# Two graph layers on one core: earlier transposes, copies graph by graph, distance rows on one engine, gates divided anew

## The chip, the cores and the metric

The kernel runs on one core of one Trainium2 chip. The metric is the device time of one execution in microseconds, the median of several. A core has four engines that compute, each with its own queue that is worked off in order: TensorE (PE in the profile, with PEld for the loading of its weights), VectorE (DVE), ScalarE (ACT) and GpSimd (POOL). SyncE (SP) issues most of the DMA transfers; ScalarE and GpSimd issue some too. An engine that waits for a semaphore holds up everything behind it in its queue.

## The reference

There are 64 graphs of 256 nodes with 256 features each, all float32. Layer 0 normalises the adjacency by the degrees, multiplies it with the features and a weight, and ends in a residual and a layer norm. Layer 1 has three branches on the result x: a convolution branch with 17 taps along the nodes, a message branch whose weights come from distances, and a gated unit (GRU) over both:

```python
h = d_inv_sqrt * adj * d_inv_sqrt + alpha_eff * I          # layer 0
x = layernorm(x + (h @ x) @ W.T + b)
c = relu(bn1(conv1x1(x)))                                   # layer 1, convolution
x_conv = relu(bn2(conv17(c)) + x)
s = x @ w_se.T + b_se                                       # layer 1, messages
A = exp(-(|s_n|^2 + |s_m|^2 - 2 s_n . s_m))
x_nmp = A @ relu(x @ w_msg.T + b_msg)
r, z = sigmoid(...), sigmoid(...)                           # layer 1, gates
n = tanh(gi_n + r * gh_n)
x = layernorm(x + (1 - z) * n + z * x)
```

## The kernel before, in words

The convolution over 17 taps is done by a discrete Fourier transform over overlapping stretches of 48 nodes, eight stretches a graph. The 64 graphs are taken in four groups of Q = 16 so that the 128 partitions are filled (16 graphs by 8 stretches). For each group four kinds of work follow one another, and work of other groups is set beside them:

- `graphs`: for each graph a generator `layer0` (two graphs ahead) and a generator `layer1`, cut into pieces by `yield`. `layer1` transposes x1 (`p_x1T`, L419) and copies it to `xn` (L420), multiplies it by the 1x1 convolution (`p_conv1`, L428) and the message weight (`p_msg`), transforms h forward (`p_dft`, L463) and copies the spectrum into the tile V (L468). Then it makes the distances: two rows are transposed into one PSUM bank (`p_rows`), `dist_l` is copied out of its lower half by ScalarE (L478) and `dist_r` out of its upper half by VectorE (L480), and `p_dist` (L487), Exp, a product with the adjacency (L489) and `p_nmp` (L494) follow. The result `xn` goes to memory. `PLACES` says after which piece of `layer1` a piece of `layer0` or of a filler ("other") is put.
- the products (`products`, L518): the spectra of V times those of the filters, on TensorE, in 12 steps. Their results overwrite V, of which M is another view.
- the inverse transform (`real_transform`, `complex_begin`, `complex_end`): on VectorE alone, in many small operations on M. `output` writes the result of each frequency pair to memory (`xc_d`, L705).
- the gates (`gates`, `gru`): for each graph the convolution result is loaded, transposed (`p_xcT`, L764), summed on GpSimd (L775 to L780), and multiplied by the gate weights (`p_rz`, L796, and `p_n`, L833).

What stands beside what is written by hand. While the products of a group run, `begin`, the first graphs of the next group, is taken a few pieces a step; as V is not free then, these AHEAD graphs (12 of the second group, 6 of the later ones) put their spectra into a second tile V2. While `complex_end` runs, `paced` puts pieces of it between the marked VectorE operations of the main work, RATES pieces for a mark:

```python
RATES = (1.2, 0.85, 0.85, 1.35)
...
run(paced(begin, end, RATES[q]))
```

After `complex_end` and the graphs ahead, four copies of ScalarE bring V2 into V (L1032), each a quarter of the frequencies of all graphs ahead at once. Then the other graphs of the group run, with the first EARLY = 4 gates of the group before as fillers; the other 12 ("late") are kept for the next products and the next inverse transform. After the last inverse transform come the 16 gates of the last group alone.

A scheduler may still move an instruction past a neighbour on its engine, so that the order of the instructions is near that of the program but not the same.

Of the kernel before, what the change touches and what calls it, by code (L numbers as in the profile page):

```python
# [14 lines left out]
P = 128  # L15
# [11 lines left out]
def kernel(  # L27
# [27 lines left out]
    nc = tc.nc  # L55
    B, N, D = x.shape
# [351 lines left out]
        nc.scalar.dma_start(x1_d[g // Q][g % Q].rearrange("(c p) d -> p c d", p=P), x1)  # L408
        yield

    def layer1(g, V, place):

        x1, adjT = X1.pop(g), ADJT.pop(g)
        xn = work.tile([P, 2 * DCH, N], F32, name="xn")
        x1T = xn[:, :DCH]
        p = bank("p_x1T").rearrange("p (k n) -> p k n", k=DCH)
        for k in range(DCH):
            for c in range(NCH):
                nc.tensor.transpose(p[:, k, c * P : (c + 1) * P], x1[:, c, k * P : (k + 1) * P], ident)  # L419
        nc.scalar.copy(x1T, p)  # L420

        yield

        h = work.tile([P, NCH, D + NSE], F32, name="h", bufs=1)
        for c in range(NCH):
            p = bank("p_conv1")[:, : D + NSE]
            for k in range(DCH):
                nc.tensor.matmul(  # L428
                    p, x1T[:, k, c * P : (c + 1) * P], wc1[:, k, :], start=k == 0, stop=k == DCH - 1
                )  # L430
            mark(nc.vector.tensor_tensor(h[:, c, :], p, bc1, op=ALU.add))
        nc.scalar.activation(h[:, :, :D], h[:, :, :D], AF.Relu)  # L432

        s3 = h[:, :, D:]
        cols = scols.rearrange("p c (q r) -> p c q r", r=32)
        nc.vector.tensor_copy(cols[:, :, :, :NSE], s3.unsqueeze(2).to_broadcast([P, NCH, 4, NSE]))
        sq3 = small.tile([P, NCH, NSE], F32, name="sq3")
        nc.vector.scalar_tensor_tensor(sq3, s3, -1.0, s3, op0=ALU.mult, op1=ALU.mult)
        nsq = small.tile([P, NCH], F32, name="nsq")
        nc.vector.tensor_reduce(nsq, sq3, AX.X, ALU.add)  # L440
        nc.vector.tensor_scalar(
            cols[:, :, 2:4, NSE], nsq.unsqueeze(2).to_broadcast([P, NCH, 2]), 0.5, None, op0=ALU.mult
        )
        yield
        msg = work.tile([P, NCH, D], F32, name="msg", bufs=1)
        p = bank("p_msg").rearrange("p (c d) -> p c d", c=NCH)
        for c in range(NCH):
            for k in range(DCH):
                nc.tensor.matmul(  # L449
                    p[:, c, :], x1T[:, k, c * P : (c + 1) * P], wmsg[:, k, :], start=k == 0, stop=k == DCH - 1  # L450
                )
        mark(nc.vector.tensor_tensor(msg, p, bmsg_t.unsqueeze(1).to_broadcast([P, NCH, D]), op=ALU.add))  # L452
        nc.scalar.activation(msg, msg, AF.Relu)
        yield


        mid = GT // 2
        for k in range(DCH):
            p = bank("p_dft")

            for c, t0, t1 in ((0, 0, mid + 1), (1, mid - 1, GT)):
                first = t0 + 1 - c * mid
                nc.tensor.matmul(  # L463
                    p[:, t0 * FL : t1 * FL], h[:, c, k * P : (k + 1) * P],
                    fwd[:, first : first + t1 - t0, :].rearrange("p t f -> p (t f)"),
                    start=c == 0, stop=True, skip_group_check=c == 1,
                )
            nc.scalar.copy(  # L468
                V[:, :, k, place * GT : (place + 1) * GT],
                p[:, : GT * FL].rearrange("p (t f) -> p f t", f=FL),  # L470
            )

        yield
        p = bank("p_rows")
        for c in range(NCH):
            nc.tensor.transpose(p[:, c * P : (c + 1) * P], scols[:, c, :], ident)
        dl = work.tile([64, N], F32, name="dist_l", bufs=1)
        nc.scalar.copy(dl, p[0:64, :N])  # L478
        dr = work.tile([64, N], F32, name="dist_r", bufs=1)
        nc.vector.tensor_copy(dr, p[64:P, :N])  # L480
        yield

        aT = work.tile([P, NCH, 2, P], F32, name="aT", bufs=1)
        for c in range(NCH):
            rows = slice(32 * c, 32 * c + 32)
            p = bank("p_dist")[:, :N]
            nc.tensor.matmul(p, dl[rows, c * P : (c + 1) * P], dr[rows, :], start=True, stop=True)  # L487
            nc.scalar.activation(aT[:, c].rearrange("p n q -> p (n q)"), p, AF.Exp, bias=nsq[:, c : c + 1], scale=2.0)  # L488
        mark(nc.vector.tensor_mul(aT, aT, adjT[:, :, 0:3:2, :]))  # L489
        yield  # L490
        p = bank("p_nmp").rearrange("p (k n) -> p k n", k=DCH)
        for k in range(DCH):
            for mc in range(NCH):
                nc.tensor.matmul(  # L494
                    p[:, k, :], msg[:, mc, k * P : (k + 1) * P], aT[:, mc].rearrange("p n q -> p (n q)"),
                    start=mc == 0, stop=mc == NCH - 1,
                )
        nc.scalar.copy(xn[:, DCH:], p)
        nc.scalar.dma_start(xn_d[g], xn)
        yield  # L500
# [3 lines left out]

    VM = freq.tile([P, FL, D], F32, name="VM")
    V, M = VM.rearrange("p f (k q) -> p f k q", k=DCH), VM

    def load_u(n, i):
        u = ustream.tile([P, DCH, D], F32, name="u")
# [362 lines left out]
    def chain(*stages):  # L872
        for stage in stages:
            yield from stage
# [13 lines left out]
    def run(stage):  # L888
        for _ in stage:
            pass  # L890
# [13 lines left out]
            yield  # L904


    PLACES = (("other",), ("layer0",), (), (), ("layer0",), ("other", "layer0"), ())

    def graphs(first, part, V, others):


        for i in part:
            load(first + i + 3)
            given = {"layer0": layer0(first + i + 2) if first + i + 2 < B else iter(()), "other": others[i]}
            for piece, _ in enumerate(layer1(first + i, V, i)):
                yield
                for name in PLACES[piece]:
                    if next(given[name], "end") != "end":
                        yield
            yield from given["other"]  # L920

    with tc.tile_pool(name="setup", bufs=1) as setup:
# [29 lines left out]
        more_weights = gate_weights()  # L952
        others = [weights(setup, i, scale2) for i in range(NPARTS)]
        others += [take(more_weights, 1) for i in range(NPARTS, Q)]
        run(graphs(0, range(Q), V, others))
        bih_t = setup.tile([P, 3 * D], F32, name="bih", tag="taps", bufs=2)
        nc.sync.dma_start(bih_t, bcast_rows(b_ih, 3 * D))
        bhh_t = setup.tile([P, 3 * D], F32, name="bhh", tag="taps", bufs=2)
# [4 lines left out]
        nc.vector.tensor_copy(bn_t[:, 0, :], bih_t[:, 2 * D :])  # L963
        nc.vector.tensor_copy(bn_t[:, 1, :], bhh_t[:, 2 * D :])
    ustream = ctx.enter_context(tc.tile_pool(name="ustream", bufs=6))
    EARLY = 4

    def open_ahead(graphs):

# [20 lines left out]
    def nothing():  # L990
        return iter(())

    RATES = (1.2, 0.85, 0.85, 1.35)


    scope, AHEAD, V2 = open_ahead(12)
    late = nothing()
    for q in range(NQ):
        first = (q + 1) * Q
        more = q + 1 < NQ  # L1000
        end = complex_end(q)
        if more:
            if q:
                others = [take(late, 3 if i % 3 == 0 else 2) for i in range(AHEAD)]
            else:
                others = [nothing() for _ in range(AHEAD)]
            begin = graphs(first, range(AHEAD), V2, others)
        sums(0)
        real = real_transform()
        for step in range(STEPS):  # L1010
            if step < 4:
                run(products(step))
            else:
                run(merge(products(step), take(real, 1)))
                run(complex_begin(step))
            if q:
                run(take(late, (0, 1, 1, 1, 1, 1, 2, 1, 2, 1, 2, 1)[step] if more else step % 2))
            else:
                run(take(begin, 3))
        run(real)  # L1020
        if not q:
            run(paced(begin, end, RATES[q]))
        elif more:
            run(paced(chain(merge(take(late, 20), take(begin, 6), 3), begin), end, RATES[q]))
        else:
            run(paced(late, end, RATES[q]))
            run(end)
        if more:
            run(late)
            run(end)  # L1030
            for f in range(0, FL, 12):
                nc.scalar.copy(V[:, f : f + 12, :, : AHEAD * GT], V2[:, f : f + 12])  # L1032
            if q == 0:
                scope.close()
                gate = ctx.enter_context(tc.tile_pool(name="gate", bufs=2))
            early = gates(q, range(EARLY))
            others = [take(early, 5 if q == 0 else 2) for _ in range(Q)]
            run(graphs(first, range(AHEAD, Q), V, others))
            run(early)
            if q == 0:  # L1040
                scope, AHEAD, V2 = open_ahead(6)
                ctx.enter_context(scope)
            late = gates(q, range(EARLY, Q))
        else:
            run(gates(q, range(Q)))

# [52 lines left out]
```

## Time and profile before

| | before |
|---|---|
| time, median of 3 | 2175.89 us (2173.8 to 2175.93) |
| span of the profiled execution | 2169.2 us |
| granted TensorE clock, mean | 0.99 |
| memory read and written | 200.62 and 103.06 MB, 140 GB/s over the span |
| first products start, groups 1 to 4 | 285.7, 645.1, 1161.7, 1668.0 us |
| last products end | about 389, 758, 1273, 1751 us |
| last store of the last inverse transform issued | 1901.6 us |

The busy time of an engine is the time in which it had an instruction in work. A wait line names the waiting engine, its output tile and its line, then whom it waited for, and then the total in us, how often, and the longest. A windows line gives for a stretch of time the busy us of each engine (and how many instructions), the granted clock, the share of the DMA engines and GB/s. In a timeline the first number is the start, the second the length; in brackets stands how long the engine had been idle and for whom. Most groups of matmuls count two entries for one matmul of the program, since each float32 product shows as two.

### The profile page before, as it was taken

To read this page: it belongs to the slowest core of one execution; us is meant where nothing else is said; L and a number is where in the kernel's file an instruction comes from. 1 tells how busy PE (TensorE), PEld (TensorE's weight loads), DVE (VectorE), ACT (ScalarE), POOL (GpSimd) and SP (SyncE) were. 2 spreads that over 40 slices of the span, in tenths; PEclk is the share of its full clock that TensorE was granted. 3 is DMA by queue.
4 is the path that set the end of the run, shared out by engine and by line. 5 is a ranking of instruction groups with operands and counts; after the bars stand their busy time and mean duration, and the time that the engine had idled before them with its cause. 6 is when DMAs were issued, how large, how long until landed. Compare 5 with 4: busy or idle time off the path is not lost. (4 is left out here: it accounts for less than half of the span.)

```text
span 2169.2 us, 29039 instructions
## 1 busy us (share of the span) xinstructions
PE 2062.6 (95%) x9805; PEld 1746.3 (81%) x9805; DVE 1551.3 (72%) x3691; ACT 833.2 (38%) x1847; POOL 664.0 (31%) x640
## 2 busy tenths in 40 slices
PE   6999999887999999999999999899999998999998
PEld 5788788766788887788888888778888887888887
DVE  5555568785568798775556989775555889977776
ACT  3665643455331122455453122346543112222222
POOL 2445310112331233313222133323231123444442
PEclk9999999999999999999999999999999999999999
DMA  4756666434347644344335654334334844444441
GB/s 120 235 193 195 199 192 213 144 122 146 93 117 226 195 118 122 107 124 120 103 98 179 204 167 115 110 115 133 101 98 124 249 117 122 124 122 104 113 105 55
DMA packets 251332, 305.65 MB, mean 141 GB/s; under 512 B 18324, under 2 KB 229864, under 8 KB 251184
## 3 DMA queue, kind: packets, MB, share of 16 engines
q1 hardware_dynamic: 183680, 200.46, 30.2%
q10 hardware_dynamic: 44480, 67.39, 8.7%
q0 software_dynamic: 23024, 35.95, 8.5%
q8 instruction: 78, 1.28, 0.2%
q14 instruction: 70, 0.57, 0.1%
HBM read 200.62 MB, written 103.06 MB: 140 GB/s over the span
## 5 line engine op out<-in xcount | busy, mean ns | idle before, releaser
L833 PE MATMUL p_n<-wn,inputs 128*128 128x256 f32 x1536 | 356.0, 385 | 10.8 <-DVE first L809 10.6
L796 PE MATMUL p_rz<-wrz,sums 128*128 128x256 f32 x1536 | 350.9, 382 | 3.2 <-POOL sums L775 2.3
L833 PEld LDWEIGHTS p_n<-wn,inputs 128*128 128x128 f32 x1536 | 289.2, 192 | 58.0 <-DVE first L809 14.3
L796 PEld LDWEIGHTS p_rz<-wrz,sums 128*128 128x128 f32 x1536 | 290.7, 191 | 48.1 <-issue 5.9
L796 PE MATMUL p_rz<-wrz,inputs 128*128 128x256 f32 x1152 | 271.7, 379 | 0.4 <-ACT inputs L766 0.4
L314 POOL TENSOR_TENSOR ln_rs<-ln_rs,neg_half 128x2 f32<-128x2 f32 x129 | 101.0, 783 | 533.8 <-DVE ln_rs L313 423.1
L796 PEld LDWEIGHTS p_rz<-wrz,inputs 128*128 128x128 f32 x1152 | 217.5, 190 | 30.3 <-ACT inputs L766 1.0
L845 ACT ACTIVATE nn<-gn 128x256 f32<-128x256 f32 x128 | 53.2, 416 | 333.3 <-DVE gn L842 333.1
L518 PE MATMUL p_k<-u,VM 128*128 128x256 f32 x736 | 175.2, 380 | 2.8 <-DMA u<-ud 1.8
L358 POOL TENSOR_TENSOR dis<-deg,neg_half 128x2 f32<-128x2 f32 x64 | 46.4, 725 | 418.1 <-DVE deg L356 410.9
L775 POOL TENSOR_TENSOR sums<-inputs 128x384 f32<-128x384 f32 x64 | 67.8, 1059 | 334.3 <-ACT inputs L766 319.9
L324 ACT ACTIVATE x_g<-x_g,ln_mr,ln_rs 128x256 f32<-128x256 f32 x128 | 70.0, 593 | 245.6 <-DVE ln_mr L322 241.8
L518 PEld LDWEIGHTS p_k<-u,VM 128*128 128x128 f32 x736 | 138.0, 190 | 24.3 <-DMA u<-ud 2.0
L428 PE MATMUL p_conv<-wc,xn 128*128 128x259 f32 x512 | 127.9, 392 | 17.6 <-ACT xn L420 17.6
L388 PE MATMUL p_hT<-adjT,x 128*128 128x256 f32 x512 | 125.9, 388 | 9.4 <-DVE msg L452 4.9
L381 POOL TENSOR_TENSOR x_t<-x_t,b_t 128x512 f32<-128x512 f32 x64 | 86.4, 1350 | 149.1 <-ACT x L380 91.7
L463 PE MATMUL p_dft<-fwd,h 128*128 128x240 f32 x512 | 117.7, 373 | 13.3 <-ACT h L432 12.1
L428 PEld LDWEIGHTS p_conv<-wc,xn 128*128 128x128 f32 x512 | 97.3, 194 | 36.8 <-ACT xn L420 22.4
L398 PE MATMUL p_out<-w,hT 128*128 128x256 f32 x512 | 123.9, 384 | 2.5 <-ACT hT L393 2.1
L489 DVE TENSOR_TENSOR aT<-aT,adjT 128x512 f32<-128x512 f32 x64 | 44.3, 692 | 110.9 <-ACT aT L488 110.9
L449 PE MATMUL p_msg<-wmsg,xn 128*128 128x256 f32 x512 | 121.6, 381 | 0.0
L494 PE MATMUL p_nmp<-aT,msg 128*128 128x256 f32 x512 | 121.1, 379 | 0.2 <-DVE aT L489 0.2
(154 smaller groups left out, 3893.6 us busy)
## 6 DMA issues: line engine op xcount, KB each, us to landing
u<-ud SPq DMA_DIRECT2D x284, 256.0 KB
xn_d<-xn ACTq DMA_DIRECT2D x64, 512.0 KB
inputs<-xn_d SPq DMA_DIRECT2D x64, 512.0 KB
ud<-u_set POOLq DMA_DIRECT2D x39, 480.0 KB, 6.0
adj_t<-in_adj_dram SPq DMA_DIRECT2D x64, 256.0 KB
x_t<-in_x_dram SPq DMA_DIRECT2D x64, 256.0 KB
x_d<-x ACTq DMA_DIRECT2D x64, 256.0 KB
xc_d<-VM SPq DMA_DIRECT2D x64, 256.0 KB
```

The lines of the kernel that those rows point to most:

```text
L314: nc.gpsimd.tensor_tensor(rs[:, : len(chunks)], rs[:, : len(chunks)], neg_half[:, : len(chunks)], op=ALU.pow)
L324: nc.scalar.activation(y[:, c, :], y[:, c, :], AF.Identity, bias=mr[:, c : c + 1], scale=rs[:, c : c + 1])
L381: nc.gpsimd.tensor_tensor(x_t, x_t, b0_t.unsqueeze(1).to_broadcast([P, NCH, D]), op=ALU.add)
L388: nc.tensor.matmul(p[:, k, :], x1[:, mc, k * P : (k + 1) * P], adjT[:, mc, 1 - mc : 3 - mc, :].rearrange("p n q -> p (n q)"), start=mc == ...
L398: nc.tensor.matmul(p[:, c, :], hT[:, k, c * P : (c + 1) * P], w0[:, k, :], start=k == 0, stop=k == DCH - 1)
L428: nc.tensor.matmul(p, x1T[:, k, c * P : (c + 1) * P], wc1[:, k, :], start=k == 0, stop=k == DCH - 1)
L449: nc.tensor.matmul(p[:, c, :], x1T[:, k, c * P : (c + 1) * P], wmsg[:, k, :], start=k == 0, stop=k == DCH - 1)
L463: nc.tensor.matmul(p[:, t0 * FL : t1 * FL], h[:, c, k * P : (k + 1) * P], fwd[:, first : first + t1 - t0, :].rearrange("p t f -> p (t f)") ...
L494: nc.tensor.matmul(p[:, k, :], msg[:, mc, k * P : (k + 1) * P], aT[:, mc].rearrange("p n q -> p (n q)"), start=mc == 0, stop=mc == NCH - 1,)
L518: nc.tensor.matmul(p[:, j * D : (j + 1) * D], v[:, k, :], u[:, k, :], start=k == 0, stop=k == DCH - 1)
L796: nc.tensor.matmul(p[:, j * D : (j + 1) * D], a[:, k], wrz[:, b, k], start=k == 0, stop=k == HALF - 1)
L833: nc.tensor.matmul(p[:, o * D : (o + 1) * D], lhsT, w, start=j == 0, stop=j == len(part) - 1)
```

## The change

There are five edits.

1. In `graphs`, the first piece of the next graph's `layer1`, which transposes x1 and copies it to `xn`, is taken as "next" at the end of the fifth piece of the present graph, ahead of `p_nmp`. Before, it stood at the start of the next graph, behind `p_nmp`. It is for having `xn` ready when `p_conv1` comes.
2. `layer1` asks `TILES[0]` where its spectrum goes. The copies from V2 to V become a generator, `copies`, which hangs on the end of `complex_end`: once the last output is out, `TILES[0]` becomes V, so that graphs which come later write there at once, and the graphs that wrote to V2 (`AWAY`) are copied one graph at a time. Before, all were copied in one block when everything else had ended.
3. `dist_r` is copied by ScalarE, as `dist_l` is.
4. EARLY becomes 4, 4 and 2: of the third group's gates only two are fillers of the last group's graphs, and 14 are kept for the last products and the last inverse transform.
5. The rates become 1.35, 0.9, 0.9 and 1.15, and in the last six steps of the first products two pieces of the graphs ahead are taken instead of three.

```diff
@@ layer1
+        if TILES[0] is not V:
+            AWAY.append(place)
...
             nc.scalar.copy(
-                V[:, :, k, place * GT : (place + 1) * GT],
+                TILES[0][:, :, k, place * GT : (place + 1) * GT],
...
-        nc.vector.tensor_copy(dr, p[64:P, :N])
+        nc.scalar.copy(dr, p[64:P, :N])
@@ graphs
-    PLACES = (("other",), ("layer0",), (), (), ("layer0",), ("other", "layer0"), ())
+    PLACES = (("other",), ("layer0",), (), (), ("layer0",), ("other", "layer0", "next"), ())
...
+        stages = {i: layer1(first + i, i) for i in part}
...
-            for piece, _ in enumerate(layer1(first + i, V, i)):
-                yield
+            for piece in range(len(PLACES)):
+                if piece or i == part[0]:
+                    next(stages[i], "end")
+                    yield
...
+            run(stages[i])
@@ the main loop
-    EARLY = 4
+    EARLY = (4, 4, 2)
...
-    RATES = (1.2, 0.85, 0.85, 1.35)
+    RATES = (1.35, 0.9, 0.9, 1.15)
...
+    def copies(V2):
+
+        waiting = list(AWAY)
+        AWAY.clear()
+        TILES[0] = V
+        for i in waiting:
+            nc.scalar.copy(V[:, :, :, i * GT : (i + 1) * GT], V2[:, :, :, i * GT : (i + 1) * GT])
+            yield
...
-        end = complex_end(q)
+        end = chain(complex_end(q), copies(V2) if more else iter(()))
...
-                run(take(begin, 3))
+                run(take(begin, 3 if step < 6 else 2))
...
-            for f in range(0, FL, 12):
-                nc.scalar.copy(V[:, f : f + 12, :, : AHEAD * GT], V2[:, f : f + 12])
...
-            early = gates(q, range(EARLY))
+            early = gates(q, range(EARLY[q]))
...
-            late = gates(q, range(EARLY, Q))
+            late = gates(q, range(EARLY[q], Q))
```

More of the change, by code (lines that the diff above doesn't have):

```diff
@@ L409, in layer0, with layer1 @@
         yield
-    def layer1(g, V, place):
+    def layer1(g, place):
         x1, adjT = X1.pop(g), ADJT.pop(g)
@@ L506 @@
     V, M = VM.rearrange("p f (k q) -> p f k q", k=DCH), VM
+    TILES, AWAY = [V], []
     def load_u(n, i):
@@ L904, in paced, with graphs @@
             yield
-    PLACES = (("other",), ("layer0",), (), (), ("layer0",), ("other", "layer0"), ())
-    def graphs(first, part, V, others):
+    PLACES = (("other",), ("layer0",), (), (), ("layer0",), ("other", "layer0", "next"), ())
+    def graphs(first, part, others):
+        stages = {i: layer1(first + i, i) for i in part}
         for i in part:
             load(first + i + 3)
-            given = {"layer0": layer0(first + i + 2) if first + i + 2 < B else iter(()), "other": others[i]}
-            for piece, _ in enumerate(layer1(first + i, V, i)):
-                yield
+            given = {
+                "layer0": layer0(first + i + 2) if first + i + 2 < B else iter(()), "other": others[i],
+                "next": stages.get(i + 1, iter(())),
+            }
+            for piece in range(len(PLACES)):
+                if piece or i == part[0]:
+                    next(stages[i], "end")
+                    yield
                 for name in PLACES[piece]:
@@ L954 @@
         others += [take(more_weights, 1) for i in range(NPARTS, Q)]
-        run(graphs(0, range(Q), V, others))
+        run(graphs(0, range(Q), others))
         bih_t = setup.tile([P, 3 * D], F32, name="bih", tag="taps", bufs=2)
@@ L1006 @@
                 others = [nothing() for _ in range(AHEAD)]
-            begin = graphs(first, range(AHEAD), V2, others)
+            TILES[0] = V2
+            begin = graphs(first, range(AHEAD), others)
         sums(0)
@@ L1035 @@
                 gate = ctx.enter_context(tc.tile_pool(name="gate", bufs=2))
-            early = gates(q, range(EARLY))
+            early = gates(q, range(EARLY[q]))
             others = [take(early, 5 if q == 0 else 2) for _ in range(Q)]
-            run(graphs(first, range(AHEAD, Q), V, others))
+            run(graphs(first, range(AHEAD, Q), others))
             run(early)
```

## The prediction

> **What bounds the kernel now.** I read the busy shares first, then who waits for whom on TensorE, then the busy time of the stages, and last the timeline around the two largest waits.
>
> ```profile
> PE 2062.6 (95%) x9805; PEld 1746.3 (81%) x9805; DVE 1551.3 (72%) x3691; ACT 833.2 (38%) x1847; POOL 664.0 (31%) x640
> ```
>
> TensorE is the bound, but 95% flatters it. In the steady last stage of the chain of waits, 42 matmul entries of L796 take 9.06 us and 24 of L833 take 5.18: 0.216 us for one of 256 columns, where the groups give a mean of 380 ns, because entries overlap. A transpose entry of half the width is taken at half, 0.108. Adding up all 9805 entries at these rates (some 8860 wide equivalents and 900 transposes) gives about 2014 us of pure work. The span of 2169 so holds 155 us of loss, and this is all that a change of order can win. Stage by stage, span less pure work: start to the first products (286) 36; first products 2; from there to the second products (389 to 645) 41; from the end of the second products to the third (758 to 1162) 23, and likewise to the fourth (1273 to 1668) 22; last stretch from 1751 on 28, of which 15 is the tail after the last matmul.
>
> ```profile
> PE p_conv L428 <- ACT xn L420: 17.6, 16, 7.6
> PE p_dist L487 <- DVE dist_r L480: 16.9, 12, 4.8
> PE p_dft L463 <- ACT h L432: 12.1, 16, 1.8
> PE p_n L833 <- DVE first L809: 10.6, 11, 2.4
> PE p_hT L388 <- DVE msg L452: 4.9, 7, 1.1
> PE p_hT L388 <- DVE adjT L370: 2.5, 3, 1.5
> ```
>
> These are TensorE's waits (total us, times, longest). The first two are what the change aims at; the fourth belongs to the gates.
>
> ```profile
> 389.00:527.00 138.00, 113.22 (x547) 89.70 (x545) 105.26 (x307) 78.58 (x172) 26.17 (x26) 0.99 0.37 120
> 758.00:862.00 104.00, 98.91 (x463) 85.56 (x462) 93.49 (x189) 28.95 (x63) 40.46 (x36) 0.97 0.44 121
> 1273.00:1377.00 104.00, 98.90 (x462) 85.53 (x461) 93.47 (x189) 28.75 (x63) 40.47 (x36) 0.97 0.45 121
> 1751.00:1902.00 151.00, 140.31 (x649) 120.81 (x648) 144.52 (x297) 33.60 (x70) 59.93 (x52) 0.99 0.43 113
> ```
>
> The four stretches in which the inverse transform (complex_end) runs beside other work; columns are PE, PEld, DVE, ACT, POOL busy. VectorE is at 76%, 90%, 90% and 96%. In the first nothing is full: it is latency. In the last VectorE is the bound.
>
> ```profile
> 522.47 4.12 ACT L1032 COPY VM<-V 128x2304 f32<-128x2304 f32 x2 [0.58 <-ACT x L324]
> 526.50 0.58 ACT L420 COPY xn<-p_x1T 128x512 f32<-128x512 f32 x1
> 527.13 3.60 PE L428 MATMUL p_conv<-wc,xn 128*128 128x259 f32 x8 [7.63 <-ACT xn L420]
> ...
> 852.41 0.43 DVE L480 COPY dist_r<-p_rows 64x256 f32<-64x256 f32 x1
> 852.90 1.22 PE L487 MATMUL p_dist<-dist_r,dist_l 32*128 32x256 f32 x4 [4.80 <-DVE dist_r L480]
> ```
>
> Here x1T sits on ScalarE behind the block of V2 copies, so conv1 starts 7.6 us late. Below, dist_l was done by 847.8, but dist_r stood behind five microseconds of gate and transform work in VectorE's queue.
>
> **What the Trainium skill says.** "Perfetto Trace Analysis", Identifying the Most-Contended Engine: busy matmul time is no measure of TensorE's headroom, weight-load busy share is better. The trace agrees: 95% against 81%. "ScalarE: Activation LUTs", What ACT_TABLE_LOAD costs: an operation with immediate scale and bias takes 186 ns + 0.833 ns per element. Copies here took 1162 ns at 1152 elements (1146 by the rule) and about 2.11 us at 2304 (2.11). "PSUM — Partial Sum Buffer", PSUM bank collisions: a compiler orders any two engines on one bank and quadrant, readers too. The two rows lie in different quadrants, yet the trace has VectorE's dist_r waiting for ScalarE's dist_l 47 times, 68.3 us: the split bought no overlap here.
>
> **The change part by part.**
> x1 transposed ahead. p_x1T (4 entries, 0.43 us) moves from behind p_nmp to before it. No work is added. Its copy (0.59 us) then runs beside p_nmp (8 entries, 1.73 us), so conv1 need not wait. The ordinary wait is 0.73 us, and about 0.17 of unfilled pipeline beside it: 15 x 0.9 = 13.5, of which waits 10. Where gates or filter weights stand between (the other 48 graphs) it was hidden already and brings nothing. The 16th, 7.63 us, is at the boundary and goes to the next part. x1T's copy now stands before the copy of p_nmp, which nobody on TensorE needs. I take 12.
>
> V2 copied graph by graph. Same elements, other cut: 10 + 5 + 5 copies of 768 elements instead of four of 2304 and eight of 1152 (the remaining graphs go straight to V). By the rule one costs 0.83 us: 20 x 0.83 = 16.6 us against 17.2. They hang on VectorE marks while the last graphs ahead still run, instead of standing in one block. They overwrite M, so the first of each batch waits for the last xc_d store; behind it in ScalarE's queue stand V<-p_dft and hT, and TensorE waits for hT. In the instruction order of the changed kernel four stand in a row, 3.3 us. I take 5 of the 7.6 us as won, and nothing at the second and third boundary, which showed no wait for ScalarE's copies.
>
> Both rows on ScalarE. 64 copies of 426 ns leave VectorE (27.3 us), 64 of about 366 (dist_l's duration) join ScalarE (23.4 us), which is 38% busy. dist_r comes 0.4 us after dist_l whatever VectorE does. hT's copy follows it, but p_hT's 1.73 us on TensorE covers both. The two waits of 4.8: 3.5 each is won, since VectorE is 90% full and will stop TensorE elsewhere: 7. The ten others, 7.3 in all, keep the chain of two copies: 0.3 each, 3. Relief of VectorE where it is nearly full (6 graphs x 0.43 in two stretches, 9 in the first): half of 9, 4. Together 14.
>
> Rates and steps. Taking 2 pieces in the last six steps moves 6 us of pure TensorE work from the first products, which lose nothing, to the first transform; neutral. There a mark now brings 1.35 transform steps, 12% more per graph, with 9 graphs for 8.4. Graphs there are 14.8 us apart (conv1 at 400.87, 415.95 ... 504.48) against 12.2 of pure work. Denser VectorE work lengthens the waits for msg and adjT (4.4 us there): cost 2.
>
> Gates 2 and 14. A gate is 66 x 0.216 + 4 x 0.108 = 14.7 us of TensorE and 10.6 of VectorE (39.1 of 54 us in the last stage). Two move from the third stretch of graphs, TensorE bound, to the last transform, VectorE bound. There 649 entries are about 138.5 us of work in 151: 9.4 gates at 16.1. With two more, VectorE needs 144.5 + 21.2 = 165.7 us for 11.4 gates, TensorE 167; with the present 4% of slack 173, against 151 + 29.4 = 180.4 if the old loss stayed. Win 7 at best; two engines that are both full stop each other, I take 4. Two gates still follow the last transform operation, as before, so the fetch of the last xc is covered. What it costs: fillers of the third stretch run out, and its last four graphs have none. Two still have layer 0 beside them (the filler-free graphs at 246 to 287 were 13.4 to 13.6 us apart, 0.9 of which goes by the x1T part): 0.5 each. Two have layer 1 alone: rows, two copies 1.1, dist, exp 0.84, product 0.69: about 2.5 us open each, the last covered partly by the products: 4 in all. Net 0.
>
> **Sum.** 12 + 5 + 14 - 2 + 4 - 4 = 29. Waits that are removed one by one in queues this full come back in part; in the four transform stretches, where most of it lies, I keep 80% of it: 23. 2175.9 - 23 = 2153.
>
> **The rivals.** (a) VectorE takes over: what speaks for it is 90% to 96% in three stretches. Then only start, boundary and the latency waits of the first stretch are won: 3 + 5 + 6, less 2 for rates and 4 for bare graphs: 8, time 2168. Against it: VectorE itself loses 27 us. (b) Slower: the copies stop ScalarE for the stores, 3 us at three boundaries, and bare graphs cost 3.5 each as a full chain, 9 + 14, and the moved gates bring nothing, against 15 won from x1T and rows: +8, time 2184. For it: four copies in a row ahead of x1T; against it: only two graphs are bare of layer 0 too. (c) Everything is won in full: conv 21, dist 17 plus its tails 2, VectorE 5, gates 7, less 4 to 8 of costs: about 42, time 2134.
>
> **How the numbers follow.** Forecast 0.62, (a) 0.16, (b) 0.08, (c) 0.14. 2136 to 2172 leaves out (b), the weak edge of (a) and the end of (c): 2 in 10. The copies' bounds (0 to 9 us) and those of the bare graphs (2 to 14) lie inside. Faster than 2171.5: the forecast, (c) and most of (a), 0.86; within 0.2% 0.06; slower 0.08.
>
> **What would show it.** Right: no TensorE wait of conv1 for xn but a few; p_dist's wait under 5 us in total, on ScalarE; graphs of the first transform under 14 us apart; the 20 copies near 0.83 us; gates in the last transform 15.3 to 15.6 us apart. Wrong: TensorE's waits for first or h grow by what conv1 and dist lost; a stop over 3 us at a copy; the last four graphs of the third stretch over 5 us slower than their work.

## The result and the profile after

The changed kernel takes 2189.31 us (median; 2185.27 to 2194.39), against 2174.85 for the kernel before on the same chip: a ratio of 1.0068, with a 95% interval of 1.0045 to 1.0091. It is slower by about 15 us where 23 us less were forecast, and 17 us above the end of the range.

The first view is the busy line of the changed kernel's page (busy us, share of the span of 2187.9 us, number of instructions).

```profile
PE 2069.7 (95%) x9805; PEld 1752.7 (80%) x9805; DVE 1526.5 (70%) x3627; ACT 861.1 (39%) x1919; POOL 668.7 (31%) x640
```

TensorE has the same 9805 entries. VectorE gave up 25 us and ScalarE took 28, near the 27.3 and 23.4 that the rows were worked out to move. So the work is what was forecast, and the time went into waiting. TensorE's waits in the changed kernel (total us, times, longest; the lines of the file moved by 2 or 3):

```profile
PE p_dft L465 <- ACT h L432: 35.1, 26, 3.5
PE p_n L836 <- DVE first L812: 13.3, 12, 3.0
PE p_hT L388 <- DVE adjT L370: 7.8, 7, 2.2
...
PE p_k L521 <- DMA u<-ud: 5.2, 5, 3.2
PE p_dist L489 <- ACT dist_r L482: 4.6, 6, 1.0
...
PE p_conv L428 <- ACT xn L420: 0.7, 1, 0.7
```

Conv1's wait fell from 17.6 to 0.7 and that of the distances from 16.9 to 4.6: both aims were reached. But the wait for h, the next one in the same graph, rose from 12.1 to 35.1, and that for adjT from 2.5 to 7.8. What the first two lost, less than a microsecond at a time, came back one product later.

The four stretches in which the inverse transform runs beside other work (us, then busy us of PE, PEld, DVE, ACT, POOL, the granted clock, the DMA share, GB/s), each from the end of the products:

```profile
395.00:542.00 147.00, 127.97 (x602) 101.37 (x602) 105.44 (x318) 86.14 (x194) 33.56 (x30) 0.98 0.42 137
762.00:866.00 104.00, 100.58 (x483) 87.42 (x482) 93.70 (x190) 30.45 (x67) 41.75 (x38) 1.00 0.46 123
1282.00:1386.00 104.00, 100.61 (x483) 87.45 (x482) 94.36 (x192) 30.45 (x67) 42.43 (x38) 1.00 0.45 120
1741.00:1916.00 175.00, 164.22 (x761) 141.18 (x760) 162.22 (x332) 40.36 (x84) 70.08 (x64) 0.99 0.42 113
```

VectorE is at 72, 90, 91 and 93% (76, 90, 90, 96 before): it got no fuller, so it did not become the bound. The time is found by setting the stages side by side. "Work moved" is pure TensorE work that the change puts elsewhere, at 0.216 us an entry.

| stage | before, us | after, us | work moved | loss |
|---|---|---|---|---|
| start to the first products | 285.7 | 300.6 | 0 | +14.9 |
| first products | 103.4 | 94.8 | -6 | -2.6 |
| to the second products | 256.0 | 254.5 | +6 | -7.5 |
| second products | 113.1 | 112.7 | 0 | -0.4 |
| to the third products | 403.5 | 407.8 | 0 | +4.3 |
| third products | 111.5 | 111.5 | 0 | 0 |
| to the last products | 394.8 | 367.9 | -31.9 | +5.0 |
| last products | 83.5 | 91.7 | +2.5 | +5.7 |
| last transform and gates | 417.7 | 446.4 | +29.4 | -0.7 |

Most of the loss lies at the start, where there is no inverse transform, no copy and no gate, and where the forecast had seen no risk: it had put 3 us of gain there. About 3 of these 14.9 us may be chance: TensorE's first conv1 comes at 32.3 us in place of 29.2, and two kernels of the experiments with the same instructions there, e9_rows_vb and e14_rows_vb_g2, differ as much (28.6 and 31.7).

The timeline of one graph of this first stage, in the changed kernel (start, length, engine and line; in brackets the idle time before and its releaser):

```profile
157.69 0.50 ACT L380 ACTIVATE x<-x_t,dis 128x256 f32<-128x256 f32 x1
...
160.05 1.92 PE L428 MATMUL p_conv<-wc,xn 128*128 128x259 f32 x8
160.58 0.73 POOL L314 TENSOR_TENSOR ln_rs<-ln_rs,neg_half 128x2 f32<-128x2 f32 x1
161.27 1.27 POOL L381 TENSOR_TENSOR x_t<-x_t,b_t 128x512 f32<-128x512 f32 x1
161.34 1.23 DVE L322 SCALAR_TENSOR_TENSOR ln_mr<-ln_mv,ln_rs 128x2 f32<-128x2 f32 x1 [2.16 <-POOL ln_rs L314]
...
162.50 0.75 DVE L431 TENSOR_TENSOR h<-p_conv,bc 128x259 f32<-128x259 f32 x2
...
164.62 0.63 ACT L432 ACTIVATE h<-h 128x512 f32<-128x512 f32 x1
...
165.31 1.89 PE L465 MATMUL p_dft<-fwd,h 128*128 128x240 f32 x8 [1.17 <-ACT h L432]
```

And the same place in the kernel before:

```profile
150.96 1.92 PE L428 MATMUL p_conv<-wc,xn 128*128 128x259 f32 x8
...
151.48 0.73 POOL L314 TENSOR_TENSOR ln_rs<-ln_rs,neg_half 128x2 f32<-128x2 f32 x1
152.25 0.16 DVE L322 SCALAR_TENSOR_TENSOR ln_mr<-ln_mv,ln_rs 128x2 f32<-128x2 f32 x1 [2.16 <-POOL ln_rs L314]
152.33 0.42 DVE L431 TENSOR_TENSOR h<-p_conv,bc 128x259 f32<-128x259 f32 x1
...
155.15 1.89 PE L463 MATMUL p_dft<-fwd,h 128*128 128x240 f32 x8
155.46 0.92 ACT L380 ACTIVATE x<-x_t,dis 128x256 f32<-128x256 f32 x2
...
156.46 1.27 POOL L381 TENSOR_TENSOR x_t<-x_t,b_t 128x512 f32<-128x512 f32 x1 [1.03 <-ACT x L380]
```

The reader is to follow L380 and L381. In layer 0, ScalarE scales x (L380), and only then may GpSimd add the bias to x_t (L381). With the early transpose the scaling has moved ahead on ScalarE, from behind p_dft to beside p_nmp. The addition so no longer comes 4 us after the power of the layer norm (L314), but at its heels, in the very time in which VectorE makes ln_mr from that power. This operation of 128x2 elements then takes 1.23 us in place of 0.16, and ends with the addition. The bias of the convolution (L431), its ReLU (L432) and p_dft stand behind it, 1.1 us late, and TensorE waits 1.17 us. Graphs with filter weights beside them are 17.1 us apart (conv1 at 125.85, 142.96, 160.05, 177.15) where they were 16.0 (118.89, 134.93, 150.96, 166.99).

The Trainium skill has this on the page "SBUF — State Buffer", Who interferes with whom: VectorE and GpSimd share one pair of ports, a VectorE instruction with two SBUF inputs contends with a GpSimd instruction that reads SBUF, and whichever is issued first keeps the pair for its whole length. The trace agrees: ln_mr has two inputs in SBUF, starts 0.07 us after the addition, and the two end at 162.57 and 162.54.

This is one of two ways in which the early addition costs. ln_mr is stretched in nine graphs, all ahead of the first products, and TensorE's waits for h in them make 11.3 of the 35.1 us. Another 12.7 us lie in six graphs of the third and last groups that have gates beside them, 2.1 us in each, where such graphs waited 0.6 to 0.7 before. There ln_mr keeps its 0.16 us:

```profile
1026.24 1.71 POOL L381 TENSOR_TENSOR x_t<-x_t,b_t 128x512 f32<-128x512 f32 x1
1027.48 1.14 POOL L314 TENSOR_TENSOR ln_rs<-ln_rs,neg_half 128x2 f32<-128x2 f32 x1
...
1028.65 0.16 DVE L322 SCALAR_TENSOR_TENSOR ln_mr<-ln_mv,ln_rs 128x2 f32<-128x2 f32 x1 [4.08 <-POOL ln_rs L314]
...
1032.04 2.65 PE L465 MATMUL p_dft<-fwd,h 128*128 128x240 f32 x8 [2.10 <-ACT h L432]
```

The addition stands ahead of the power in GpSimd's own queue, so that the power itself comes late, and with it ln_mr and what VectorE does behind it. At this place in the kernel before the addition came last, and VectorE's sq, 0.16 us by itself, was stretched beside it:

```profile
1024.94 1.16 POOL L314 TENSOR_TENSOR ln_rs<-ln_rs,neg_half 128x2 f32<-128x2 f32 x1
...
1028.45 1.26 POOL L381 TENSOR_TENSOR x_t<-x_t,b_t 128x512 f32<-128x512 f32 x1 [2.35 <-ACT x L380]
1028.48 1.25 DVE L438 SCALAR_TENSOR_TENSOR sq<-h 128x6 f32<-128x6 f32 x1
```

### The profile page after: what moved, and what is told of

Read it like the earlier page. It is cut to its first block, busy times and chain, and to the rows that moved or that the text cites. A ratio compares the mean times of both kernels' runs of the same rounds, so it can differ in the third digit from the quotient of the medians.

```text
span 2187.9 us, 29118 instructions
## 1 busy us (share of the span) xinstructions
PE 2069.7 (95%) x9805; PEld 1752.7 (80%) x9805; DVE 1526.5 (70%) x3627; ACT 861.1 (39%) x1919; POOL 668.7 (31%) x640
## 5 line engine op out<-in xcount | busy, mean ns | idle before, releaser
L836 PE MATMUL p_n<-wn,inputs 128*128 128x256 f32 x1536 | 351.1, 382 | 13.5 <-DVE first L812 13.3
L836 PEld LDWEIGHTS p_n<-wn,inputs 128*128 128x128 f32 x1536 | 288.1, 191 | 59.3 <-DVE first L812 16.3
L314 POOL TENSOR_TENSOR ln_rs<-ln_rs,neg_half 128x2 f32<-128x2 f32 x129 | 101.7, 788 | 448.4 <-DVE ln_rs L313 379.9
L778 POOL TENSOR_TENSOR sums<-inputs 128x384 f32<-128x384 f32 x64 | 67.8, 1060 | 367.9 <-ACT inputs L769 351.0
L465 PE MATMUL p_dft<-fwd,h 128*128 128x240 f32 x512 | 120.9, 380 | 35.6 <-ACT h L432 35.1
L388 PE MATMUL p_hT<-adjT,x 128*128 128x256 f32 x512 | 131.1, 400 | 13.9 <-DVE adjT L370 7.8
L465 PEld LDWEIGHTS p_dft<-fwd,h 128*128 128x128 f32 x512 | 96.0, 193 | 55.9 <-ACT h L432 49.0
L381 POOL TENSOR_TENSOR x_t<-x_t,b_t 128x512 f32<-128x512 f32 x64 | 92.9, 1451 | 120.7 <-ACT x L380 72.1
## 6 DMA issues: line engine op xcount, KB each, us to landing
u<-ud SPq DMA_DIRECT2D x284, 256.0 KB
adj_t<-in_adj_dram SPq DMA_DIRECT2D x64, 256.0 KB
x_t<-in_x_dram SPq DMA_DIRECT2D x64, 256.0 KB
x_d<-x ACTq DMA_DIRECT2D x64, 256.0 KB
xc_d<-VM SPq DMA_DIRECT2D x64, 256.0 KB
```

What stands on the lines that cost most here:

```text
L314: nc.gpsimd.tensor_tensor(rs[:, : len(chunks)], rs[:, : len(chunks)], neg_half[:, : len(chunks)], op=ALU.pow)
L381: nc.gpsimd.tensor_tensor(x_t, x_t, b0_t.unsqueeze(1).to_broadcast([P, NCH, D]), op=ALU.add)
L388: nc.tensor.matmul(p[:, k, :], x1[:, mc, k * P : (k + 1) * P], adjT[:, mc, 1 - mc : 3 - mc, :].rearrange("p n q -> p (n q)"), start=mc == ...
L465: nc.tensor.matmul(p[:, t0 * FL : t1 * FL], h[:, c, k * P : (k + 1) * P], fwd[:, first : first + t1 - t0, :].rearrange("p t f -> p (t f)") ...
L836: nc.tensor.matmul(p[:, o * D : (o + 1) * D], lhsT, w, start=j == 0, stop=j == len(part) - 1)
```

## The experiments

Theory: the early transpose is what costs, by way of the order of the addition and of ln_mr, and a smaller part comes from the gates and the rates. Rivals: VectorE is the bound and gives nothing back whatever is won; or the copies graph by graph hold ScalarE up.

**Each part alone, in the kernel before.** `e1_x1t` is edit 1 of the change (the "next" of `PLACES`), `e8_copies` edit 2 with the rates 1.35, 0.9 and 0.9 and the steps of two pieces. The other two:

```diff
# e2_rows
-        nc.vector.tensor_copy(dr, p[64:P, :N])
+        nc.scalar.copy(dr, p[64:P, :N])
# e3_gates
-    EARLY = 4
+    EARLY = (4, 4, 2)
-    RATES = (1.2, 0.85, 0.85, 1.35)
+    RATES = (1.2, 0.85, 0.85, 1.15)
```

> The kernel before with the early transpose of x1 alone. Theory (order): with x1T ahead, the scaling of the graph after next on ScalarE slips forward beside p_nmp, the addition x_t + b on GpSimd slips in right behind the layer norm's power, and VectorE's 128x2 operation ln_mr takes 1.23 us beside it instead of 0.16; h and its relu come late and TensorE waits about 1.2 us for h at each graph that has filter weights beside it. So in the first group those graphs are 17.1 us apart, not 16.0, and the first products start at 297 to 301 us (before: 285.7); the first transform wins about 7 us; in all 2178 to 2186. Rival (ScalarE's load from dist_r is what delays h): no change of the distance, first products at 282 to 284, in all 2158 to 2165.

> The kernel before with dist_r on ScalarE alone. Theory (order): the scaling and x_t + b keep their place, graphs with filter weights stay 16.0 us apart, the two waits of 4.8 us of p_dist go; 2162 to 2170. Rival (the two copies in a row on ScalarE delay h's relu or hT): p_dft's or p_out's waits grow by 10 us or more, 2180 to 2190.

> The kernel before with the gates 4, 4, 2 and the last rate 1.15 alone. Theory: two bare graphs at the end of the last group cost about 4 us, the last products, which start with nothing behind them, about 4 to 5 more, and the last transform gives back 1; 2180 to 2186. Rival (the divided gates win in the last transform what was forecast, 4 us, and lose 4): 2172 to 2177, no difference.

> The kernel before with the copies graph by graph, the steps of 2 and the rates 1.35, 0.9, 0.9 (1.35 in the last) alone. Theory: the wait of 7.6 us at the boundary goes, denser transform work gives back about 2; 2166 to 2172. Rival (the copies stop ScalarE for the stores and the denser transform work stops h): no win or slower, 2174 to 2182.

| | us | ratio to before, 95% |
|---|---|---|
| e1_x1t | 2193.37 | 1.0084 (1.0059 to 1.0108) |
| e2_rows | 2161.26 | 0.9945 (0.993 to 0.996) |
| e3_gates | 2185.22 | 1.0051 (1.0036 to 1.0066) |
| e8_copies | 2178.97 | 1.0021 (1.0012 to 1.0029) |

The rows win 12 us and each other part loses: 20, 12 and 5 by the medians, 18, 11 and 5 by the ratios. Alone they sum to a loss of 22 to 25, and together they cost 15, so their losses overlap by some 7 to 10. e3_gates lies where its theory put it, and e2_rows 1 us below. The transpose is worse even than the theory asked, and the copies, which the theory had down for a gain, are slightly slower, as their rival said. TensorE's waits in e1_x1t:

```profile
PE p_dft L463 <- ACT h L432: 39.1, 27, 3.8
...
PE p_conv L428 <- ACT xn L420: 8.2, 2, 7.6
```

One edit makes the whole exchange: conv1 loses all its short waits (9.4 us), and h gains 27.0. The first products start at 302.8 us (285.7 before). Both ways of the loss are there: nine ln_mr of 1.23 us, and seven graphs with gates that wait 2.1 to 2.2 us for h.

**The order put back.** One line makes the scaling L380 wait in ScalarE's queue for the copy of p_adjT, in every graph and not only in the first two. It changes no work. `e4_bias` has it in the changed kernel, `e5_x1t_late` beside the early transpose alone, `e6_rest` in the changed kernel with the gates 4 and 12 again and the last rate 1.35.

```diff
-        with tc.issue_after(copied.ins) if g < 2 else ExitStack():
+        with tc.issue_after(copied.ins):
```

> The changed kernel, with one line: the scaling of x_t on ScalarE is queued behind the copy of p_adjT in every graph, not only in the first two, which puts x_t + b on GpSimd behind the next filter store as before the change. Theory (order): ln_mr is back at 0.16 us in the first group, graphs with filter weights 16.0 us apart, first products at 282 to 286 us instead of 300.6, in all 2170 to 2177. Rival (it is x1T's copy itself, or ScalarE's load): p_dft still waits 1.2 us a graph, 2186 to 2192.

> The kernel before with the early transpose and the one line that queues the scaling of x_t behind the copy of p_adjT. Theory (order: only the place of x_t + b made the early transpose dear): no 1.23 us ln_mr in the first group, graphs with filter weights 16.0 us apart, first products at 282 to 286, conv1's waits gone but for the one at the boundary; 2160 to 2170, 20 to 33 us under the early transpose alone. Rival (an early transpose moves the wait to h wherever it goes): 2176 or more, p_dft's wait over 20 us.

> The changed kernel with the one line, and with the gates 4, 4, 4 and the last rate 1.35 of before. Theory (parts add up): 2173.5 less the 12 that the gates alone cost: 2158 to 2165, the last products starting with no wait for u, and the last two graphs of the last group under 1 us of bare waits each. Rival (with the other edits the moved gates cost nothing): 2170 to 2177.

Measured: e4_bias 2173.52 (ratio 1.0002, 0.9994 to 1.0011), e5_x1t_late 2174.34 (1.0005, 0.9994 to 1.0016), e6_rest 2167.66 (0.9972, 0.9961 to 0.9983), 3 us above the theory. The order alone is worth 16 to 19 us by the medians, about as much as was lost: ln_mr is at 0.16 us everywhere, and the graphs with gates wait 0.9 us for h. The start is back too, within what it scatters by (286.4 us in e4_bias, 288.9 in e5_x1t_late, 291.6 in e6_rest). But the early transpose still brings nothing, where the theory gave it some 4 to 14 us; e5_x1t_late lies between its two expectations, with 18.3 us of waits for h. The timeline of e5_x1t_late, in the first transform, shows a part of why:

```profile
436.93 1.93 POOL L381 TENSOR_TENSOR x_t<-x_t,b_t 128x512 f32<-128x512 f32 x1 [3.29 <-issue]
...
437.66 1.61 DVE L370 SCALAR_TENSOR_TENSOR adjT<-ident,adeg,adjT 128x128 f32<-128x128 f32 x2
...
439.15 1.97 PE L388 MATMUL p_hT<-adjT,x 128*128 128x256 f32 x8 [1.49 <-DVE adjT L370]
```

The addition now meets VectorE's two operations on adjT instead. They took 0.60 us in the kernel before at 155.69, take 1.61 here, and TensorE waits 1.49. Counting the additions beside which a VectorE operation takes over half as long again as its median, one finds 28 of 64 in the kernel before, 33 in the changed one, 31 in e1_x1t and 25 in e5_x1t_late, and 27 to 32 us of such excess in each. The order hardly changes how much is held; it changes what is held, and so whether TensorE waits for it.

**The addition taken off GpSimd.** `e7_nobias` is e1_x1t without L381: it leaves out the bias of layer 0. The others do the same addition on VectorE: in the kernel before (`e12_before_vb`), there with the rows on ScalarE (`e9_rows_vb`), with the early transpose as well (`e10_x1t_rows_vb`), and in the changed kernel (`e11_after_vb`).

```diff
-        nc.gpsimd.tensor_tensor(x_t, x_t, b0_t.unsqueeze(1).to_broadcast([P, NCH, D]), op=ALU.add)
+        nc.vector.tensor_tensor(x_t, x_t, b0_t.unsqueeze(1).to_broadcast([P, NCH, D]), op=ALU.add)
```

> The kernel before with the early transpose, with the addition of layer 0's bias to x_t on GpSimd left out (its output lacks that bias); ScalarE's order stays that of the early transpose, with the scaling ahead. Theory (GpSimd's x_t + b is what VectorE's ln_mr waits beside): ln_mr at 0.16 us everywhere, first products at 282 to 287. Rival (ScalarE's early scaling or the transpose itself delays h): first products still at 297 or later.

> The kernel before with dist_r on ScalarE, and x_t + b on VectorE in place of GpSimd. Theory (x_t + b on GpSimd holds VectorE for its 1.3 us wherever it falls; on VectorE it costs 0.7): below the rows alone, 2150 to 2160. Rival (VectorE is too full for 44 us more): at or above the rows alone, 2161 to 2172.

> The same with the early transpose as well. Theory: with nothing long on GpSimd beside the layer norm the early transpose keeps what it wins; ln_mr at 0.16 us, first products at 282 to 287; 2143 to 2153, 5 to 8 below the kernel without it. Rival (the transpose only moves the wait to h, adjT or the rows): the same as without it within 4 us.

> The whole change with x_t + b on VectorE. Theory: the 1.23 us ln_mr is gone, first products at 282 to 287 in place of 300.6; the moved gates still cost 12: 2155 to 2168 in all. Rival (what the change costs lies in ScalarE's queue): p_dft's wait stays over 25 us, 2183 or more.

> The kernel before with x_t + b on VectorE alone. Theory: there x_t + b mostly fell where VectorE was idle, so little is won: 2162 to 2174. Rival (VectorE is too full): 2176 to 2190.

| | us | ratio to before, 95% |
|---|---|---|
| e7_nobias (one run) | 2152.5 | |
| e12_before_vb | 2161.58 | 0.9943 (0.9928 to 0.9957) |
| e9_rows_vb | 2149.48 | 0.9893 (0.9876 to 0.991) |
| e10_x1t_rows_vb | 2149.35 | 0.9889 (0.9875 to 0.9904) |
| e11_after_vb | 2161.7 | 0.9943 (0.9924 to 0.9962) |

In e7_nobias ln_mr is back at 0.16 us and the first products start at 285.8, as the theory said. e11_after_vb lies in its theory's range, e9_rows_vb and e12_before_vb just below theirs, and for e10_x1t_rows_vb the rival holds. Without the addition the early transpose alone falls from 2193.4 to 2152.5: 41 us, for an operation that takes 1.3 us a graph on an engine at 30%. On VectorE the addition gives 28 us to the changed kernel, and 12 to the kernel before: it was stopping VectorE there too, unseen. Two groups, first of before and then of e12_before_vb (busy us, mean ns, idle time before):

```profile
L438 DVE SCALAR_TENSOR_TENSOR sq<-h 128x6 f32<-128x6 f32 x64 | 17.7, 276 | 0.0
```

```profile
L381 DVE TENSOR_TENSOR x_t<-x_t,b_t 128x512 f32<-128x512 f32 x64 | 47.1, 736 | 15.4 <-ACT x L380 13.9
...
L438 DVE SCALAR_TENSOR_TENSOR sq<-h 128x6 f32<-128x6 f32 x64 | 10.1, 158 | 0.0
```

VectorE takes on 47.1 us of additions, yet its busy time grows by only 13 (1551.3 to 1564.5), as other operations get shorter; sq alone, which stands right ahead of the norms that feed the distances, gives 7.6: seven of its 64 took 1.25 us before. A held operation counts as busy, so that no wait line names the stop; it shows in the durations. What part of the 12 us comes from a shorter queue of GpSimd (664.0 us busy before, 579.4 here) these runs do not separate. The Trainium skill, "Perfetto Trace Analysis", Optimizing Scalar/DVE Operations, warns that moving work between VectorE and GpSimd may not help because of this port; here keeping it on GpSimd cost 12 us, in a kernel whose VectorE was the busier of the two.

e10 against e9 shows the early transpose with the addition off GpSimd: no gain (a difference of 0.1 us; the intervals leave room for some 4 either way). TensorE's waits in e9_rows_vb:

```profile
PE p_conv L428 <- ACT xn L420: 17.9, 17, 7.3
...
PE p_dft L463 <- ACT h L432: 9.3, 15, 1.2
```

and in e10_x1t_rows_vb:

```profile
PE p_dft L463 <- ACT h L432: 20.5, 18, 3.7
...
PE p_conv L428 <- ACT xn L420: 8.3, 2, 7.6
```

Conv1 loses 9.6 us and h gains 11.2. Conv1 may start early, but h needs conv1's end, two operations of VectorE and one of ScalarE, and only p_msg and p_adjT are there to cover them. The wait is that of a chain, and the edit moved it along. This pair is not free of GpSimd, though: in e10 the addition on VectorE is itself held 18 times out of 64, 1.3 to 1.5 us in place of 0.69 (in e9 it is 4 times), beside GpSimd's work on u_set and sums. e7_nobias, which has no addition at all, tells about how much that matters: against e12_before_vb conv1's waits are 8.3 in place of 18.4 us and those for h 17.6 in place of 9.8. So most of what conv1 wins, some 8 of 10 us, comes back without any addition; the rest may be the held addition's doing.

**The gates and the rates.** e11_after_vb (2161.7) is still 12 us behind e10_x1t_rows_vb. `e13_after_vb_ungates` takes the gates out of e11 (4 and 12, last rate 1.35); the others change only these constants of e9_rows_vb:

```diff
# e13_after_vb_ungates
-    EARLY = (4, 4, 2)
+    EARLY = (4, 4, 4)
-    RATES = (1.35, 0.9, 0.9, 1.15)
+    RATES = (1.35, 0.9, 0.9, 1.35)
# e14_rows_vb_g2: EARLY = (4, 4, 2)
# e15_rows_vb_g6: EARLY = (4, 4, 6), last rate 1.65
# e16_rows_vb_g2_r115: EARLY = (4, 4, 2), last rate 1.15
# e17_rows_vb_r115: last rate 1.15
```

> The changed kernel with x_t + b on VectorE, and the gates divided 4 and 12 again with a last rate of 1.35. Theory (the division of the gates makes the whole of the 12 us between 2161.7 and 2149.35): 2147 to 2153. Rival (the copies graph by graph and the steps of 2 keep costing about 5 us, as they did alone): 2154 to 2158. Third (the division costs nothing once the addition is moved): 2160 to 2163.

> The kernel before with the rows on ScalarE and x_t + b on VectorE (2149.5), and only the gates divided 2 and 14, the last rate left at 1.35. Theory (bare graphs and the two later gates cost 10 us and over whatever the rate): 2157 to 2164. Rival (it was the lower rate of 1.15 that cost in the earlier run): 2148 to 2153.

> The same kernel (2149.5) with the gates of the third group divided the other way, 6 and 10, last rate 1.65. Theory (a late gate is dearer than an early one by some 5 us): 2140 to 2147. Rival (4 is the right number: fillers cover the last graphs already, and the last transform, on VectorE, has fewer gates beside it and gets no shorter): 2149 to 2160.

> The kernel before with the rows on ScalarE, x_t + b on VectorE, the gates divided 2 and 14 and the last rate at 1.15. Theory (the lower rate carries half of the cost: the last transform is spread over more of the gates, and ends later): 2156 to 2162. Rival (the rate is nothing, the division is all): 2152 to 2155.

> The same kernel with the gates 4 and 12 as before, and only the last rate lowered to 1.15. Theory (the lower rate leaves transform work over when the late gates are used up, so that VectorE runs it with TensorE idle): 2154 to 2162. Rival (the rate is nothing): 2148 to 2152.

| | us | ratio to before, 95% |
|---|---|---|
| e13_after_vb_ungates | 2154.35 | 0.9907 (0.9892 to 0.9923) |
| e14_rows_vb_g2 | 2153.4 | 0.9907 (0.9888 to 0.9926) |
| e15_rows_vb_g6 | 2155.75 | 0.9911 (0.9892 to 0.9929) |
| e16_rows_vb_g2_r115 | 2159.05 | 0.993 (0.9914 to 0.9946) |
| e17_rows_vb_r115 | 2161.36 | 0.9937 (0.9918 to 0.9956) |

Of the 12 us, the gates with their rate make about 7, and the copies with the other rates the remaining 5, as the rival for e13 said and as in e8_copies; the intervals of e13 and e10 overlap, so the 5 rests on e8_copies. Neither 2 nor 6 early gates beats 4, but their intervals overlap with that of e9_rows_vb (0.9876 to 0.991), so that no loss is shown either. For e14 neither expectation holds (it lies between them), for e15 the rival; e16 and e17 lie in the ranges of their theories. What is clear is the rate: with 4 and 12 gates, 1.15 costs 12 us by the medians (10 by the ratios). TensorE at the end of the last transform, in e17_rows_vb_r115:

```profile
1898.81 1.89 PE L796 MATMUL p_rz<-wrz,inputs 128*128 128x256 f32 x8
1911.17 1.11 PE L764 MATMUL p_xcT<-ident,xc_g 128*128 128x128 f32 x4 [10.48 <-DMA xc_g<-x_d]
```

and in e9_rows_vb, VectorE's last operation of the transform and TensorE's first of the last group's gates:

```profile
1876.86 0.75 DVE L704 SCALAR_TENSOR_TENSOR VM<-turn,VM 128x256 f32<-128x256 f32 x2
...
1899.39 0.60 PE L764 MATMUL p_xcT<-ident,xc_g 128*128 128x128 f32 x4
```

At 1.35 the transform is done 22 us before TensorE turns to the last group's gates, which covers the store and the fetch of xc. At 1.15 its last VectorE operation (at 1899.65) falls at the end of the late gates, and TensorE stands idle 10.5 us for the transfer. The denser rate had not made the gates slower, either: the ten gates of that stretch are 16.4 us apart at 1.35 and 16.1 at 1.15. With 14 late gates no such wait shows, so in the changed kernel the price of the division is another one, told below; whether 1.15 costs anything there is not settled, e14 and e16 being too close.

The fastest are e9_rows_vb and e10_x1t_rows_vb, 1.1% under the kernel before and 1.8% under the changed one. e9_rows_vb differs from the kernel before in two lines: the copy of dist_r, which is part of the change, and the addition, which is not.

## Why the prediction was wrong

**x1 transposed ahead: the step that failed.** It said that no work is added and 12 us are won. It cost 20 us alone (18 by the ratio). The step counted the ordinary wait of conv1 at 0.9 us times 15, and asked of the copy of x1T only who waits for it. For the 48 graphs with gates or filter weights between it said that the edit brings nothing. Just there it lost. Two things were left out. First, the order: the edit let L380 go ahead, and with it GpSimd's addition, onto ln_mr in the graphs with filter weights and ahead of the power in graphs with gates. That the addition's place is the cause is shown by e4_bias, e5_x1t_late, e7_nobias and e11_after_vb; how the loss divides between the two ways is read from the traces only. Second, even with the addition away the wait mostly moves to h (e7_nobias, e9 and e10), so the term is about 0 and not 12. The sentence on what would show it wrong, that waits for h grow by what conv1 lost, is what came: 23.0 us for conv1's 16.9.

**Both rows on ScalarE: right.** 14 was said, 12 came in e2_rows, and 12 again between e12_before_vb and e9_rows_vb. The waits of p_dist fell to 4.6 us (under 5 was said) and the copy takes 368 ns (366 was said).

**V2 copied graph by graph, with the rates: wrong by 8 us.** 5 less 2 was said, and e8_copies measured 5 slower. The size of the copies was right:

```profile
L1014 ACT COPY VM<-V 128x768 f32<-128x768 f32 x20 | 15.5, 836 | 3.3 <-DMA xc_d<-VM 2.3 <-DVE trz L818 1.0
```

836 ns where 830 was said, and 2.3 us of waiting for stores in all, so rival (b)'s stop of 9 us fell. Conv1's boundary wait of 7.6 us went (the longest is 2.3 in e8_copies). But graphs in the first transform came 14 to 17 us apart in the changed kernel (conv1 at 399.14, 415.15, 429.03, 444.04, 458.56 and later at 488.13, 505.38, 522.61), not under 14, and adjT is waited for there. Which of the copies, the steps or the rates makes the 5 us was not taken apart.

**Gates 2 and 14: net 0 was said; a loss of 11 to 12 came in e3_gates, and of 7 in the changed kernel with the addition moved.** The bare graphs were sized well: the third stretch of e3_gates got shorter by 25.8 us for 29.4 of work, 4 us lost as the prediction had it. Two terms failed. The last transform was to give 4 back and gave none: the last stretch of e3_gates is 31.1 us longer for 29.4 of work. In the changed kernel gates are 16.3 us apart there (from 1745 to 1908), much as before (16.4, from 1755 to 1903), and not 15.3 to 15.6. The prediction had VectorE as the bound of this stretch. VectorE falls from 96 to 93%, and where e17_rows_vb_r115 gives it 15% less transform work a gate than e9_rows_vb, the gates come closer by only 0.3 us, so its load is not what spaces them. What does was not found. And the last products, for which the sum had no term, are 3.3 us longer in e3_gates and 5.7 beyond their work in the changed kernel. The last graph runs there with nothing beside it:

```profile
1632.26 1.92 PE L428 MATMUL p_conv<-wc,xn 128*128 128x259 f32 x8
...
1638.73 0.70 PE L489 MATMUL p_dist<-dist_r,dist_l 32*128 32x256 f32 x4 [0.99 <-ACT dist_r L482]
...
1641.08 3.42 PE L496 MATMUL p_nmp<-aT,msg 128*128 128x256 f32 x8 [1.06 <-DVE aT L491]
...
1644.34 1.92 PE L428 MATMUL p_conv<-wc,xn 128*128 128x259 f32 x8
```

From conv1 to conv1 it is 12.1 us for some 8.3 of work, and the graph after it runs on into the products.

**The rivals.** (a) VectorE takes over: not in any stretch (72 to 93% busy). (b) came nearest in time, 2184, but by other means: its stop for stores is not there, its bare graphs cost 4 and not 14, and the transpose, which it had as a gain, is the loss. The factor of 80%, meant for waits that come back, was a discount on a gain. It allowed for no term that changes its sign, and so the range ended at 2172. Two readings in the prediction do not hold, though nothing came of them. The gains of (c), 21, 17, 2, 5 and 7, less 4 to 8, make 44 to 48 and not 42. And the trace does not bear out that the weight-load share of 81% tells TensorE's room better than the matmul share of 95%: the prediction's own estimate of pure work, 2014 of 2169 us, is 93%.

## What to carry to other kernels

When an edit moves an instruction, look at what moves with it on the other engines, and at what each GpSimd operation then runs beside: a small VectorE operation in a dependent chain was held here for the whole length of a GpSimd operation, with the profile calling it busy, and a long operation moved ahead in GpSimd's queue made the short one behind it late. The durations of one form, shortest against longest, show the first; the order of the queue shows the second. Here waits of under a microsecond at the head of a chain of dependent products were not won by starting the head sooner, as the next link had no cover. Filler work is a stock: before a rate or a division is changed, ask what stands beside the last unit of each stage and whether a transfer behind it is still covered.

## What the runs showed of the hardware

A 128x2 VectorE operation of 0.16 us took 1.23 us beside a GpSimd addition, and two on adjT 1.61 in place of 0.60. GpSimd's addition, 1.27 us in the median, took 1.93 beside VectorE's work in e5_x1t_late. The same addition takes 0.69 us on VectorE in the median, and 1.3 to 1.5 beside some of GpSimd's operations (e10_x1t_rows_vb). Sixty-four of them moved from an engine that is 31% busy to one that is 72% busy made the kernel before 12 us faster.
